# Counting ranks partly on ScalarE, a more even split of row sums, and group matrices six steps ahead in a four-layer graph kernel

## Chip, cores and metric

One Trainium2 chip, one of its cores. The metric is the device time of one execution in microseconds, given as the median of several runs. Float32 inputs and output; TensorE's fp32 matmuls run as two passes in the profile ("x2" for one matmul of the source).

## The reference

Four graph layers over one adjacency matrix `adj` (2708 x 2708, sparse, non-negative) and 2708 nodes with 128 features. Each layer ends in `x = layernorm(x + layer(x))`. Layer 0 is a normalised graph convolution, layer 2 a hyperbolic one, layer 3 sums neighbours over the signs of `adj`. What the change touches is layer 1:

```python
XW = x @ W
s_col, s_row = XW @ a[0, :f], XW @ a[0, f:]
den = exp(leaky_relu(s_row[:, None] + s_col[None, :], 0.01))
num = A @ den
att = where(num != 0, den / num, 0)
H = A @ (att @ XW)
```

`den` depends on two numbers per node only, and `leaky_relu` on the sign of their sum. So once the nodes are sorted by these numbers, a row of `num` differs from its neighbour by few nodes, and a dense product can be replaced by work on groups of sorted nodes.

## The kernel before

Nodes lie in 22 tiles of 128 (`NT`), columns in six blocks (`NB`) of 512, the last one 148 wide. The kernel first reads `adjT` in blocks and does layer 0 (L866), keeping the lower part of the blocks in SBUF (`kept`). Then, block by block, it normalises (`norm_roots`, `normed`), multiplies by the weights (`projected`: TensorE at L1001, ScalarE's copies at L1010 and L1011) and clamps the two numbers per node (`clamped`).

Layer 1 needs the ranks of the nodes. Column tiles 1 to 3 serve as 384 samples (`samples`, first two of them replaced by sentinels). `count` (L1051) compares the samples with one value per partition, on VectorE: for each of 22 node tiles and each of the two numbers `i` one instruction of 128 x 384 adds the comparison's result to `counts[:, i, :]`, and writes the number of hits per node, running, to `counted`. `below_s` is the sum of `counts` over the partitions, as a row and as three columns, by TensorE (L1190 to L1195). From it VectorE finds for every sample how far back a group may reach (`lim`, `prev`, L1209), and in a serial search of 26 steps (L1239) the limits `v` of 26 groups (`GM`). From `v` and the counts per node (`upto`) come one-hot matrices `oh`, TensorE's prefix sums `low` (L1288, L1298), a slot per node (`slot`), and two lists of nodes by group: for each node tile VectorE makes a 128 x 128 one-hot `ohs` (L1326) and TensorE multiplies it into `list` (L1328), first for `i` = 0 (it gives `row_i`, the rows of `adjT` to gather), then for `i` = 1.

Beside that runs the whole sum: `whole_sum` (L803) adds `exp` of one number times every row of `adj`. One row tile is nine narrow matmuls (M = 1) into four column groups of two PSUM banks: blocks 0 to 3 in the first bank, block 4 in four pieces of `q4` = 160 columns (the last 32) and block 5 with 148 in the second. `sum_rows(n)` places `n` of the 22 row tiles between other work on TensorE. Order of the row tiles: those of block 0, of blocks 4 and 5, then 1, 2, 3. The upper blocks were overwritten, so the blocks of rows 0 to 3 are fetched again (`fetch_next`, DMA at L824 on SP's queue) into places that come free when a block of rows has been summed; `x_d` (L1515) and `xw_d` (L1012) are written by the same queue.

`queued(...)` makes the instructions of an engine keep the order in which they are written; elsewhere a scheduler orders them.

Then follows `grouped_attention`: 52 steps `q` (26 groups for each half of the nodes). A step gathers 128 rows (`gather`, GpSimd's indirect DMA, L1415, three steps ahead), multiplies them by a group matrix into `num` (L1464), takes `ln` and `exp` on ScalarE, and adds `xw_g` times `att` into `uacc` two steps later (L1491). The first two partitions carry a running sum from step to step (L1467; the first from `carry0`, L1446). A group matrix is a transpose on TensorE (L707) into one of two PSUM buffers `ps`, which ScalarE empties with a Relu (L708). The same two buffers hold two of every five tiles of `num`. The first three matrices lie in `samples` (`w_first`, `FIRST` = 3), the others in `w_all`, made three steps ahead.

A flag (`good`, `added_up`, `checked`) selects at the end a general path if the data do not fit the assumptions of the fast one.

Of the kernel before, what the change touches and what calls it, by code (L numbers as in the profile page):

```python
# [29 lines left out]
NS = len(SAMPLES) * P  # L30
CAP = 126
FIRST = NS // P
GM = 26
SENTINEL = 1.0e29
EMPTY = -1.0e5
# [17 lines left out]
def tiles(b):  # L53
    return range(b * (BW // P), min(NT, (b + 1) * (BW // P)))
# [3 lines left out]
def kernel(  # L58
# [51 lines left out]
    def iota(name, n, base, step, channel, dt=F32):  # L110
        nc.gpsimd.iota(iota_i[:, :n], pattern=[[step, n]], base=base, channel_multiplier=channel)
        t = const.tile([P, n], dt, tag=name, name=name)
        nc.gpsimd.tensor_copy(t, iota_i[:, :n])
        return t

    iota_b = iota("iota_b", P, 0, 1, 0, BF16)
    part_f = iota("part_f", 1, 0, 1, 1)
    node_z = iota("node_z", NT, -N, P, 1)
# [599 lines left out]
    nc.gpsimd.memset(counts, 0.0)  # L718
    counted = col.tile([P, 2, NT + 1], F32, tag="counted", name="counted")
    nc.gpsimd.memset(counted[:, :, 0:1], 0.0)  # L720

# [60 lines left out]

    e1 = c_tile("e1")
    e2 = c_tile("e2")
    q4 = 160
    order = [0, NB - 2, NB - 1, *range(1, NB - 2)]
    steps = iter([(d, i) for d in order for i in range(len(tiles(d)))])

# [1 line left out]
    sums_of += [(4, i * q4, min(BW, (i + 1) * q4), 32 * i, 1, 0) for i in range(4)]  # L792
    sums_of += [(5, 0, width(5), 96, 1, BW - 3 * q4)]
    tot = []

    def whole_sum(n):
        if not tot:
# [43 lines left out]
    with tc.tile_pool(name="tri", bufs=1) as tp:  # L841
# [174 lines left out]
        def clamped(c):  # L1016
            span = node_span(c)
            with queued(DVE):
                nc.vector.tensor_scalar(
                    rcl[:, :, span].rearrange("p i t -> p t i"),  # L1020
                    rc[:, span, ::-1],
                    RC_MAX,
                    -RC_MAX,
                    op0=ALU.min,
                    op1=ALU.max,
                )
                nc.vector.tensor_copy(cmp_v[:, 0, span], rcl[:, 0, span])
                nc.vector.tensor_scalar(cmp_v[:, 1, span], rcl[:, 1, span], -1.0, None, op0=ALU.mult)
                if c == NB - 1:
                    for i in range(2):  # L1030
                        nc.vector.tensor_add(cmp_v[:, i, span], cmp_v[:, i, span], pad_big[:, span])
            with queued(ACT):
                nc.scalar.activation(e1[:, span], rcl[:, 0, span], AF.Exp)
            if c == 0:
                ps = ps_tile("samples_ps")
                with queued(PE):
                    for q, t in enumerate(SAMPLES):
                        nc.tensor.transpose(
                            ps[:, q * P : (q + 1) * P], rcl[:, 0, t : t + 1].to_broadcast([P, P]), ident
                        )  # L1040
                with queued(DVE):
                    nc.vector.tensor_copy(samples, ps[:, :NS])
                    nc.vector.memset(samples[:, 0:1], -SENTINEL)
                    nc.vector.memset(samples[:, 1:2], SENTINEL)

        def count(c, a=0, b=8):


            with queued(DVE):
                for t, i in itertools.islice(itertools.product(tiles(c), range(2)), a, b):  # L1050
                    nc.vector.scalar_tensor_tensor(  # L1051
                        counts[:, i, :],
                        samples,
                        cmp_v[:, i, t : t + 1],
                        counts[:, i, :],
                        op0=ALU.is_gt,
                        op1=ALU.add,
                        accum_out=counted[:, i, t + 1 : t + 2],
                    )

        def sum_rows(n):
            with queued(PE):
                return whole_sum(n)
# [80 lines left out]
                count(c - 1, 0, 4 if c < NB - 2 else 1)  # L1144
        last_products(NB - 1, 0)
        summed_up(NB - 1)
        count(NB - 3, 1, 3)
        norm_roots(NB - 2)
        norm_roots(NB - 1)
        sum_rows(1)  # L1150
        count(NB - 3, 3, 6)
        normed(NB - 2)
        sum_rows(1)
        normed(NB - 1)
        count(NB - 3, 6)
# [12 lines left out]
    with ctx_keep:  # L1168
# [11 lines left out]
        with tc.tile_pool(name="sort", bufs=1) as st_p:  # L1180
# [4 lines left out]

            lim = srt([P, 2, len(SAMPLES)], "lim")
            prev = srt([P, 2, len(SAMPLES)], "prev")
            below_s = [acc_tile(4 + i, f"below{i}") for i in range(2)]
            with queued(PE):
                nc.tensor.matmul(below_s[0][:, :NS], lhsT=ones_b, rhs=counts[:, 0, :], start=True, stop=True)  # L1190
            for i in range(2):
                if i:
                    nc.tensor.matmul(below_s[i][:, :NS], lhsT=ones_b, rhs=counts[:, i, :], start=True, stop=True)
                for q in range(len(SAMPLES)):
                    nc.tensor.matmul(  # L1195
                        below_s[i][:, NS + q : NS + q + 1],
                        lhsT=counts[:, i, q * P : (q + 1) * P],
                        rhs=ones_b[:, 0:1],
                        start=True,
                        stop=True,  # L1200
                    )

            for i in range(2):
                nc.vector.tensor_scalar(
# [51 lines left out]


            upto = srt([P, 2, NT], "upto")
            nc.vector.tensor_sub(upto, counted[:, :, :NT], counted[:, :, 1:])
# [48 lines left out]
            for i in range(2):  # L1308
# [8 lines left out]
                    )  # L1317
                nc.vector.tensor_reduce(slot[:, i, :], pos[i], AX.X, ALU.add)
                nc.vector.tensor_scalar(slot[:, i, :], slot[:, i, :], 2.0, None, op0=ALU.add)
                ps = ps_tile(f"list{i}")  # L1320
                sum_rows(2)
                for t in range(NT):
                    if i == 0 and t in (8, 16):
                        sum_rows(1)
                    ohs = srt([P, P], f"ohs{i}_{t}", BF16, 10, "ohs")
                    nc.vector.tensor_scalar(ohs, iota_b, slot[:, i, t : t + 1], None, op0=ALU.is_equal)  # L1326
                    with queued(PE):
                        nc.tensor.matmul(  # L1328
                            ps[:, : 6 * GM],
                            lhsT=ohs,  # L1330
                            rhs=val[i][:, t, :, :].rearrange("p n g -> p (n g)"),
                            start=(t == 0),
                            stop=(t == NT - 1),
                        )
# [51 lines left out]
    gs = c_tile("gs", 1)  # L1386

    def added_up():
        below0, okb = (c_tile(n, 1) for n in ("below0", "okb"))
# [12 lines left out]
    def grouped_attention(u_sb, rows_g):  # L1402
        adj_h = adjT.rearrange("k (h w) -> (k h) w", h=2)
        chunks = [(0, BW), (BW, 2 * BW), (2 * BW, HALF)]
        with tc.tile_pool(name="main", bufs=1) as mp:
# [79 lines left out]
            def aggregate(q):  # L1485
# [12 lines left out]
                if g == GM - 1:  # L1498
                    for c, (ca, cb) in enumerate(chunks):
# [474 lines left out]
```

## Time and profile before

| | |
|---|---|
| runs, us | 899.6, 901.1, 905.04; median 901.1 |
| profiled execution, us | 904.86, of which the span 903.1 |
| PE / DVE / ACT / POOL busy | 94% / 61% / 43% / 23% |
| mean granted TensorE clock | 0.973 |
| whole sum, ranks, search and lists | from about 164 to 226 us |
| grouped attention, first to last matmul | from 226.57 to 474 us |
| layers 2 and 3 | from 474 us to the end |

PE is TensorE, DVE VectorE, ACT ScalarE, POOL GpSimd, SP the sync engine whose queue issues most transfers; PEld is TensorE's weight load, which overlaps PE. PEclk is the share of full TensorE clock that was granted, and DMA share the mean busy share of the 16 DMA engines (it can pass 1 where packets overlap). The chain of waits is followed back from the last instruction, each step to what released it; a line of it gives start, duration, engine, tile and source line. "[1.70 <-DMA B]" behind an instruction in a timeline means that the engine was idle for 1.70 us before it and was released by that transfer.

### The profile page before, as it was taken

The numbers are of one execution on the slowest core, as the hardware profiler recorded it, in microseconds if no ns is written. First come the engines' busy times: TensorE is split into PE (matmuls) and PEld (weight loads), VectorE is DVE, ScalarE is ACT, GpSimd is POOL, SyncE is SP. The second block draws the span as 40 slices with busy tenths as digits, with TensorE's granted clock in tenths as the row PEclk, the third lists the DMA queues.
The fourth block names the chain that finished last, engine by engine and source line by source line (L and its number), as shares of the span: only waits on it lengthen the run. The fifth ranks groups of instructions, "written<-read, shape, count | busy, mean of one in ns | idle before, by whom it ended". The sixth has DMA issues, their size and how long they took to land.

```text
span 903.1 us, 9464 instructions
## 1 busy us (share of the span) xinstructions
PE 846.5 (94%) x3268; PEld 430.0 (48%) x3268; DVE 555.2 (61%) x1189; ACT 388.6 (43%) x681; POOL 206.1 (23%) x176
## 2 busy tenths in 40 slices
PE   3699999698899999999999999989999899999996
PEld 3254454335344445444454444534444555555555
DVE  4777548988788888889971226375644564233313
ACT  3776433215787777777761115273332221000000
POOL 5221000101888885776500000000000000000000
PEclk9799999889899999999999999999999999999997
DMA  9995684596596555445534776496764565463410
GB/s 341 366 356 209 120 248 141 180 383 217 185 380 202 161 150 160 141 154 154 154 121 167 267 269 229 133 336 239 264 224 131 208 215 198 144 253 142 162 39 19
DMA packets 95979, 184.30 MB, mean 204 GB/s; under 512 B 6446, under 2 KB 23551, under 8 KB 95668
## 3 DMA queue, kind: packets, MB, share of 16 engines
q1 hardware_dynamic: 85700, 143.82, 46.2%
q0 software_dynamic: 8352, 37.76, 13.0%
q10 hardware_dynamic: 1872, 2.04, 0.7%
q8 instruction: 28, 0.46, 0.2%
q14 instruction: 27, 0.22, 0.1%
HBM read 179.33 MB, written 4.28 MB: 203 GB/s over the span
## 4 chain that ended last, share of the span: by engine, by line
PE 84%; DMA 9%; DVE 4%; ACT 2%; issue 0%; SPq 0%; DVEq 0%; ACTq 0%
PE a L1584 22%; PE num L1464 13%; PE uacc L1491 13%; PE a L1863 12%; PE a L866 9%; PE a L1872 6%; DMA A<-in_adjT_dram 4%; DMA B<-in_adjT_dram 3%; PE t L803 1%; DMA cb<-in_adjT_dram 1%; PE pp L1821 1%; DVE counts L1051 1%; PE mx L1691 1%; DMA rows_g<-in_adjT_dram,row_i 1%; PE su L251 0%
## 5 line engine op out<-in xcount | busy, mean ns | idle before, releaser
L1415 POOL DMA_INDIRECT rows_g<-in_adjT_dram,row_i x52 | 130.8, 2515 | 90.2 <-PE num L1464 41.2
L1469 ACT ACTIVATE ln<-num,inval,occ_l 128x512 f32<-128x512 f32 x156 | 107.4, 724 | 53.4 <-DVE rows_g L1467 49.4
L1863 PE MATMUL a<-cb,ut 128*128 128x512 f32 (+2 forms) x264 | 125.8, 559 | 1.1 <-DMA cb<-in_adjT_dram 1.1
L1491 PE MATMUL uacc<-att,xw_g 128*128 128x512 f32 (+1 forms) x312 | 126.3, 542 | 0.0
L1872 PE MATMUL a<-mask,node 128*128 128x512 f32 (+2 forms) x264 | 120.3, 537 | 0.7 <-DVE mask L1851 0.7
L1464 PE MATMUL num<-rows_g,w_all 128*128 128x512 f32 (+1 forms) x276 | 113.8, 545 | 0.8 <-ACT ln L1469 0.8
L1584 PE MATMUL a<-cb,q_b 128*128 128x512 f32 (+2 forms) x264 | 111.6, 561 | 1.8 <-DMA cb<-in_adjT_dram 1.8
L866 PE MATMUL a<-A,q_b 128*128 128x512 f32 (+2 forms) x264 | 105.9, 549 | 1.6 <-DMA A<-in_adjT_dram 1.6
L1584 PE MATMUL a<-cb,xw 128*128 128x512 f32 (+2 forms) x264 | 107.3, 550 | 0.0
L1467 DVE COPY rows_g<-num 2x512 f32<-2x512 f32 x150 | 88.0, 612 | 15.4 <-PE num L1464 14.1
L1491 PEld LDWEIGHTS uacc<-att,xw_g 128*128 128x128 f32 x312 | 59.1, 190 | 59.0 <-issue 50.0
L1483 DVE TENSOR_TENSOR att<-att,ln 128x1354 f32<-128x1354 f32 x52 | 80.5, 1548 | 2.0 <-ACT ln L1479 2.0
L1464 PEld LDWEIGHTS num<-rows_g,w_all 128*128 128x128 f32 x276 | 49.5, 190 | 54.0 <-issue 38.9
L1872 PEld LDWEIGHTS a<-mask,node 128*128 128x128 f32 (+1 forms) x264 | 48.5, 193 | 49.4 <-issue 47.6
L230 ACT ACTIVATE sq_l<-s 128x512 f32<-128x512 f32 (+1 forms) x11 | 6.6, 604 | 148.2 <-DVE s L1881 116.7
L1479 ACT ACTIVATE ln<-ln 128x1354 f32<-128x1354 f32 x52 | 69.3, 1333 | 1.7
L1851 DVE TENSOR_SCALAR mask<-cb 128x3072 fp32r<-128x3072 f32 (+5 forms) x24 | 33.5, 1395 | 59.1 <-PE a L1872 58.6
L866 PEld LDWEIGHTS a<-A,q_b 128*128 128x128 f32 (+1 forms) x264 | 45.8, 190 | 49.8 <-issue 46.4
L1584 PEld LDWEIGHTS a<-cb,q_b 128*128 128x128 f32 (+1 forms) x264 | 45.1, 192 | 46.9 <-issue 42.8
L1584 PEld LDWEIGHTS a<-cb,xw 128*128 128x128 f32 (+1 forms) x264 | 45.1, 190 | 46.5 <-issue 46.5
L1074 ACT ACTIVATE xw<-A 128x2048 f32<-128x2048 f32 (+3 forms) x36 | 57.0, 1582 | 7.9 <-DMA b_s<-in_b_dram 4.3
L1456 DVE TENSOR_SCALAR att<-q_b,gj_l 128x1354 f32<-128x1354 f32 x52 | 48.2, 927 | 12.7 <-PE uacc L1491 12.6
(445 smaller groups left out, 900.6 us busy)
## 6 DMA issues: line engine op xcount, KB each, us to landing
cb<-in_adjT_dram SPq DMA_DIRECT2D x15, 2816.0 KB
cb<-in_adjT_dram SPq DMA_DIRECT2D x15, 2560.0 KB
A<-in_adjT_dram SPq DMA_DIRECT2D x25, 1024.0 KB
B<-in_adjT_dram SPq DMA_DIRECT2D x18, 1024.0 KB
cb<-in_adjT_dram SPq DMA_DIRECT2D x3, 814.0 KB
cb<-in_adjT_dram SPq DMA_DIRECT2D x3, 740.0 KB
ut<-in_adjT_dram SPq DMA_DIRECT2D x2, 1024.0 KB
A<-in_adjT_dram SPq DMA_DIRECT2D x5, 296.0 KB
```

Source lines behind the costliest of these rows:

```text
L866: nc.tensor.matmul(acc[c][:, :w], lhsT=z[:kw, k, :], rhs=t[:kw, i, :w], start=c not in begun, stop=(d == NB - 1 and k == NT - 1), skip_gro ...
L1074: checks[d, c] = nc.scalar.activation(below[:, :nt, :w], t[:, :nt, :w], AF.Relu, scale=-1.0, accum_out=neg_sum[:, NB * c + d : NB * c + d ...
L1415: got = nc.gpsimd.indirect_dma_start(out=gat[q], out_offset=None, in_=adj_h, in_offset=bass.IndirectOffsetOnAxis(ap=row_i[:, h, g : g + 1] ...
L1464: nc.tensor.matmul(num[:, : cb - ca], lhsT=w, rhs=gat[q][:, ca:cb], start=True, stop=True)
L1467: nc.vector.tensor_copy(gat[q + 1][0:2, ca:cb], num[0:2, : cb - ca])
L1469: nc.scalar.activation(ln_n[q][:, ca:cb], num[:, : cb - ca], AF.Ln, scale=occ_l[:, g : g + 1], bias=inval[:, g : g + 1],)
L1479: nc.scalar.activation(ln_n[q], ln_n[q], AF.Exp, scale=-1.0)
L1483: nc.vector.tensor_mul(att[q], att[q], ln_n[q])
L1491: nc.tensor.matmul(uacc[h][c][:, : cb - ca], lhsT=xw_g[:, g, :], rhs=att[q][:, ca:cb], start=(g == 0), stop=(g == GM - 1),)
L1584: nc.tensor.matmul(acc[:, :w], lhsT=weights[:kw, k, :], rhs=pc[:kw, t, :w], start=(k == 0), stop=(k == NT - 1),)
L1863: nc.tensor.matmul(acc[:, :w], lhsT=edge[:ke, k, :], rhs=pc[:ke, t, :w], start=(k == 0), stop=False, skip_group_check=True,)
L1872: nc.tensor.matmul(acc[:, :w], lhsT=node[:kw, k, j, :], rhs=mask[:kw, t - ma, :w], start=False, stop=(k == NT - 1 and j == 1), skip_group_ ...
```

## The change

Four things, in one diff:

- For node tiles 12 to 21 (blocks from `SIGNS` = 3 on) the counts of the second number (`i` = 1), ten in all, are made by ScalarE: `Sign(samples - v)` into a bf16 tile `sg` (three buffers), with the sum per node in `signed`. TensorE adds each `sg`, times one half, to `below_s[1]` as a row and three columns; the constant by which signs and counts differ falls out of the comparison with `lim`, and is put back in `upto`. The calls of `count`, `sum_rows` and the new `signs` and `signs_summed` are interleaved anew.
- `q4` is 165: the second bank's four column groups get 165 columns each (block 5: 17 + 148).
- The one-hot tiles `ohs` have four buffers instead of ten, and the flag also asks for the largest slot.
- Group matrices: three more before the loop, then six steps ahead instead of three, behind `group_xw` in the text.

```diff
+SIGNS = 3
+    half_b = const.tile([P, 1], BF16, tag="half_b", name="half_b")
+    nc.gpsimd.memset(half_b, 0.5)
...
-    q4 = 160
+    q4 = (N - 4 * BW) // 4
...
+    def below_sum(i, src, w):
+        parts = [(slice(0, NS), w, src)]
+        parts += [(slice(NS + q, NS + q + 1), src[:, q * P : (q + 1) * P], w[:, 0:1]) for q in range(len(SAMPLES))]
+        for at, lhsT, rhs in parts:
+            nc.tensor.matmul(below_s[i][:, at], lhsT=lhsT, rhs=rhs, start=i not in begun_s, stop=True,
+                             skip_group_check=True)
+            begun_s.add(i)
...
+                if c >= SIGNS:
+                    nc.vector.tensor_scalar(neg_v[:, span], cmp_v[:, 1, span], -1.0, None, op0=ALU.mult)
...
-                for t, i in itertools.islice(itertools.product(tiles(c), range(2)), a, b):
+                for t, i in itertools.islice(itertools.product(tiles(c), range(2 - (c >= SIGNS))), a, b):
...
+        def signs(c, a=0, b=4):
+            for t in tiles(c)[a:b]:
+                sg = col.tile([P, NS], BF16, tag="sg", name=f"sg_{t}", bufs=3)
+                with queued(ACT):
+                    nc.scalar.activation(
+                        sg, samples, AF.Sign, bias=neg_v[:, t : t + 1], accum_out=signed[:, t : t + 1]
+                    )
+                sides.append(sg)
+        def signs_summed(n):
+            if not below_s:
+                below_s.extend((acc_tile(4, "below0"), acc_tile(3, "below1")))
+            for _ in range(n):
+                sg = sides.pop(0)
+                with queued(PE):
+                    below_sum(1, sg, half_b.to_broadcast([P, P]))
...
-        count(NB - 3, 1, 3)
+        count(NB - 3, 1, 2)
         norm_roots(NB - 2)
         norm_roots(NB - 1)
         sum_rows(1)
-        count(NB - 3, 3, 6)
+        signs(NB - 3, 0, 2)
+        count(NB - 3, 2)
         normed(NB - 2)
         sum_rows(1)
         normed(NB - 1)
-        count(NB - 3, 6)
         projected(NB - 2)
         projected(NB - 1)
-        sum_rows(2)
+        signs(NB - 3, 2)
+        sum_rows(1)
+        signs_summed(2)
         clamped(NB - 2)
+        signs(NB - 2)
         count(NB - 2)
         clamped(NB - 1)
+        signs(NB - 1)
         count(NB - 1)
+        signs_summed(2)
+        sum_rows(1)
+        with queued(PE):
+            below_sum(1, counts[:, 1, :], ones_b)
+        signs_summed(6)
...
+            nc.vector.tensor_scalar(upto[:, 1, ns:], signed[:, ns:], -0.5, -0.5 * NS, op0=ALU.mult, op1=ALU.add)
...
+                if i:
+                    nc.vector.tensor_reduce(most, slot.rearrange("p i t -> p (i t)"), AX.X, ALU.max)
...
-                    ohs = srt([P, P], f"ohs{i}_{t}", BF16, 10, "ohs")
+                    ohs = srt([P, P], f"ohs{i}_{t}", BF16, 4, "ohs")
...
+        nc.vector.tensor_scalar(fit, most, float(P - 1), None, op0=ALU.is_le)
+        nc.vector.tensor_mul(good, good, fit.to_broadcast([P, NT]))
...
+            with queued(PE, ACT):
+                for g in range(FIRST, FIRST + 3):
+                    group_matrix(w_all, g)
...
                     if q + 3 < GM:
+                        group_xw(q + 3, behind)
+                    if q + FIRST + 3 < GM:
                         with queued(PE, ACT):
-                            group_matrix(w_all, q + 3)
-                        group_xw(q + 3, behind)
+                            group_matrix(w_all, q + FIRST + 3)
```

More of the change, by code (lines that the diff above doesn't have):

```diff
@@ L720 @@
     nc.gpsimd.memset(counted[:, :, 0:1], 0.0)
+    neg_v = col.tile([P, NT], F32, tag="neg_v", name="neg_v")
+    signed = col.tile([P, NT], F32, tag="signed", name="signed")
+    most = col.tile([P, 1], F32, tag="most", name="most")
     xw = const.tile([P, NT, F], F32, tag="xw", name="xw")
@@ L794 @@
     tot = []
+    sides, below_s, begun_s = [], [], set()
+    def below_sum(i, src, w):
+        parts = [(slice(0, NS), w, src)]
+        parts += [(slice(NS + q, NS + q + 1), src[:, q * P : (q + 1) * P], w[:, 0:1]) for q in range(len(SAMPLES))]
+        for at, lhsT, rhs in parts:
+            nc.tensor.matmul(
+                below_s[i][:, at],
+                lhsT=lhsT,
+                rhs=rhs,
+                start=i not in begun_s,
+                stop=True,
+                skip_group_check=True,
+            )
+            begun_s.add(i)
     def whole_sum(n):
@@ L1059, in count @@
                     )
+        def signs(c, a=0, b=4):
[4 more added lines that the diff above has]
+                        sg, samples, AF.Sign, bias=neg_v[:, t : t + 1], accum_out=signed[:, t : t + 1]
+                    )
+                sides.append(sg)
[6 more added lines that the diff above has]
+                    below_sum(1, sg, half_b.to_broadcast([P, P]))
         def sum_rows(n):
@@ L1187 @@
             prev = srt([P, 2, len(SAMPLES)], "prev")
-            below_s = [acc_tile(4 + i, f"below{i}") for i in range(2)]
             with queued(PE):
[L1190 to L1201, printed above, removed]
+                below_sum(0, counts[:, 0, :], ones_b)
             for i in range(2):
@@ L1258 @@
             upto = srt([P, 2, NT], "upto")
-            nc.vector.tensor_sub(upto, counted[:, :, :NT], counted[:, :, 1:])
+            ns = tiles(SIGNS)[0]
+            nc.vector.tensor_sub(upto[:, 0], counted[:, 0, :NT], counted[:, 0, 1:])
+            nc.vector.tensor_sub(upto[:, 1, :ns], counted[:, 1, :ns], counted[:, 1, 1 : ns + 1])
+            nc.vector.tensor_scalar(upto[:, 1, ns:], signed[:, ns:], -0.5, -0.5 * NS, op0=ALU.mult, op1=ALU.add)
             vs = srt([P, GM + 1], "vs")
@@ L1388, in added_up @@
     def added_up():
-        below0, okb = (c_tile(n, 1) for n in ("below0", "okb"))
+        below0, okb, fit = (c_tile(n, 1) for n in ("below0", "okb", "fit"))
+        nc.vector.tensor_scalar(fit, most, float(P - 1), None, op0=ALU.is_le)
+        nc.vector.tensor_mul(good, good, fit.to_broadcast([P, NT]))
         nc.vector.tensor_reduce(below0, neg_sum, AX.X, ALU.add)
```

## The prediction

> **What bounds the kernel now.** I read the page's shares, then the chain of waits in order of time, then a table of 3 us windows, then the timelines of the engines from 160 to 260 us, where all that the diff touches lies.
>
> ```profile
> PE 846.5 (94%) x3268; PEld 430.0 (48%) x3268; DVE 555.2 (61%) x1189; ACT 388.6 (43%) x681; POOL 206.1 (23%) x176
> PE 84%; DMA 9%; DVE 4%; ACT 2%; issue 0%; SPq 0%; DVEq 0%; ACTq 0%
> ```
> TensorE carries the span. VectorE's 61% is an average and says nothing of the stretch in question. The chain there:
> ```profile
> 170.84 4.37 DVE counts L1051 x16
> 175.81 1.78 DVE counts L1051 x6
> 178.80 4.42 PE t L803 x30
> 187.65 12.43 DMA B<-in_adjT_dram
> ...
> 202.19 12.26 DMA B<-in_adjT_dram
> 214.49 0.41 PE t L803 x2
> 217.35 2.45 PE t L803 x30
> 219.80 0.30 PE list L1328 x3
> 220.10 5.41 DMA rows_g<-in_adjT_dram,row_i
> 226.57 3.79 PE num L1464 x4
> ```
> The counts are on the chain from 170.8 to 177.6, then it goes over to the refetched blocks B of the whole sum, and the first gather leaves at 220.10, when the last whole-sum row is through TensorE (row_i was ready at 218.72). The windows (us, then busy PE, PEld, DVE, ACT, POOL, PEclk, DMA share, GB/s):
> ```profile
> 174.00:177.00 3.00, 0.00 (x0) 0.00 (x0) 2.96 (x16) 0.32 (x2) 1.26 (x4) 0.82 1.09 285
> 180.00:183.00 3.00, 3.00 (x32) 1.17 (x24) 2.18 (x10) 0.00 (x0) 0.00 (x0) 0.54 1.05 392
> 186.00:189.00 3.00, 3.00 (x45) 1.25 (x33) 2.82 (x11) 0.60 (x1) 0.00 (x0) 1.00 1.05 387
> 204.00:207.00 3.00, 3.00 (x44) 2.33 (x43) 3.00 (x6) 2.79 (x19) 0.00 (x0) 1.00 1.06 388
> 213.00:216.00 3.00, 2.81 (x35) 1.11 (x38) 2.34 (x15) 0.00 (x0) 0.00 (x0) 1.00 0.12 33
> ```
> From 174 to 213 us the DMA engines are full at about 388 GB/s: 13 blocks of 1 MB and three thin ones. So two things run side by side: VectorE's counts, ranks and group search, and this transfer stream. TensorE waits for the stream at 199.16 (1.70 us), 200.12 (0.51) and 214.49 (0.19); the last landing ends the stream at 214.44.
>
> **What the Trainium skill says.** "ScalarE: Activation LUTs", What ACT_TABLE_LOAD costs: an ACTIVATE with a pointer bias takes about 280 ns plus 0.833 ns per column, 0.60 us at 384. The trace has 302 ns for L1703 (128 columns, no pointer), started every 0.29 us with its accumulator read; adding 256 columns (0.21) and a pointer (0.09) gives 0.60 as well. The same section puts a table switch at 2.66 us; the built order of the changed kernel holds no further table load among the signs and exponentials, so I price none. "TensorE: Matmul & The Clock Gate", Part 1: an idle array falls to half clock and comes back after sustained work. The trace agrees: idle for 4.67 us before 177.73, then PEclk 0.50 to about 182.7, and the 36 matmuls of two rows take 4.49 us instead of 2.52. "DMA: Bandwidth & Descriptors", Rules for kernel authors: all queues share the same 16 engines, so an earlier issue does not widen a full stream; the windows above show it full.
>
> **The change part by part.**
>
> *Counts.* Eight counts start 0.54 us apart (170.81 to 175.13). Ten go, 5.4 us of VectorE, and three small neg_v operations of about 0.1 come. Before 166.7 one count only lengthens an existing wait for ScalarE's roots, so VectorE reaches x (L992) at 167.74 instead of 168.28: 0.54 earlier. The last count ends at about 174.4 instead of 178.1. Next late are the signs: ScalarE is free from 165.7, takes two signs to 166.9, the projection's copies (L1010, L1011) to 170.45, then eight signs of 0.60 with the three buffers of sg handed back by TensorE: I get the last at about 176.3. TensorE's sums cost 0.27 us each at full clock (below at L1190 and three columns take 0.54 at half clock): 2.7 us, in the former idle. So lim starts at about 177.1 instead of 178.35; with a warm TensorE the two rows ahead of prev_ps no longer hold it, and the search (26 steps of 0.655, L1239) starts about 2.2 us earlier and ends at 199.2 instead of 201.4.
>
> *What that buys.* Nothing, I think. Behind the search come oh and low on TensorE, queued behind rows and rb (203.75) that wait for B landings. The end of the stream counts. It starts with B1_2 behind x_d and two writes of xw_d on SP's queue. These start 0.54 earlier, so their bytes are through at about 174.3 instead of 174.8. But B1_2 may only be issued when row 4 of block 0 is summed, and this row now stands behind four sums, of which the fourth needs a sign that needs the first one's buffer: row start 172.45 instead of 171.8, issue 173.4 instead of 172.72. Somewhat above half a microsecond passes from issue to data (x_d: 169.20, DMA busy from about 169.8). Ends between 0.55 earlier and 0.3 later: I take 0.
>
> *Rows dealt 165 instead of 160 and 180.* A row takes 1.21 us (54 matmuls, 3.62) for 692 columns in its two turns; 15 fewer are 0.026, and six rows lie after the stall at 200: 0.15 us gained.
>
> *ohs, four buffers instead of ten.* VectorE makes one in 0.163 to 0.182 us, TensorE's list takes 0.082 (x8 in 0.66), and VectorE restarts 0.28 after a group's first list matmul (214.83 to 215.11). With eight ready the group costs 0.66; with four ready, 0.28 + 4 x 0.175 + 0.2 = 1.2. The first group of list0 grows inside the wait for the landing at 214.44; the second adds 0.5, the last (six) 0.33. So whole sum and gather end 0.83 later. For list1 TensorE has 22 to take: before, twelve were still to be made when it began (219.73 to the copy at 222.53, 2.80 us), now 18, six more at 0.175: 1.05. If VectorE ran at TensorE's full round trip instead it would be far more (rival 3); below nothing it cannot be, as nothing is left out. The added maximum of slot (about 0.2) lies in VectorE's wait.
>
> *Group matrices.* Ahead of the first numerators stood four (L707, L708), now seven: three pass through two PSUM buffers at ScalarE's pace, 0.40 to 0.45 us each. The fourth is out of TensorE at 226.03, so the seventh at about 227.3, against the start of num at 226.57: 0.75. The gather that covers this (landing 225.51, carry copy to 226.53) moves only by the 0.83, while the matrices move by 0.83 + 1.05; the cover is gone. In the loop three steps (20 to 22) lose their matrix: 0.11 each (246.02 to 246.13), and step 21 its stall of 0.28 (num x6 takes 2.72 at 326.13 instead of 2.44): 0.61 gained. Steps 1, 6, 11 and 16 keep theirs, as one matrix per step still takes a PSUM buffer of num. POOL and SP issue in the same order, so nothing moves past their queues.
>
> Sum: 0 - 0.15 + 0.83 + 1.05 + 0.75 - 0.61 = +1.87 us. Two operations of fit come in step 39 of the loop, in VectorE's idle time; behind the loop no engine's order differs, so the rest should shift whole. The profiled execution took 904.86 (span 903.1); with 1.9 more, 906.8. It lies 3.8 above the median of the runs, 901.1; the forecast for a median is 903.0.
>
> **Rivals.**
> Rival 1, not slower: the stream follows its releases. The chain puts the issue at 187.65 on TensorE's rb, which the earlier search and a warm clock bring about 2.2 us forward. If that moved the landings, the sum is 1.87 - 2.2 = -0.3: 900.8. For it: the chain's own edge. Against: share 1.05 and 387 GB/s on both sides of 187.65. It decides from the point where the share dips before that issue; if the earlier start of x_d also moves the stream by its 0.55, 900.2.
> Rival 2: signs take 0.75 instead of 0.60, or the sums hold block 0's last row for another 1.5 us; the full stream then ends that much later: +3.4, 904.5. For it: the buffer ring ties ScalarE and TensorE together. Against: ScalarE is idle for 4.03 and 4.15 us there.
> Rival 3: four buffers run at the round trip. One turn is about 0.175 + 0.25 + 0.2 = 0.63 us; were it not overlapped, 18 + 6 matrices would lose 24 x 0.45 = 10.8 us: 914. Against: 0.63 over four buffers is 0.157, still below VectorE's own pace.
> That the signs are not on ScalarE is excluded: the built order shows all ten.
>
> **How the numbers follow.** Forecast 0.55 (+0.5 to +3), rival 1 0.25, rival 2 0.15, rival 3 0.05. The predicted time is the forecast's, 903.0. The range leaves out rival 3, reaches down past rival 1 and up past rival 2, and takes in the 0.3% by which runs of one kernel differ (899.6 to 905.04): 898.5 to 907.5. A change of 1%, 9 us, is about what a measurement of this kernel can tell from none. Only rival 3 passes it, 0.05; faster by that much, 0.02, would need more than the whole 5.4 us of counts; within 1%, 0.93.
>
> **What would show it.** Right: counts end near 174.4 and lim starts near 177; last B landing within 0.5 us of 214.4; DMA share above 1 throughout; first gather near 221; list1 taking about 3.9 us; first num near 229; one stall fewer in the loop, then everything about 2 us later. Wrong: a landing 2 us earlier (rival 1) or later (rival 2), list1 above 6 us (rival 3), or a difference that first arises after 480 us.

## The result, and the profile after

The changed kernel's median is 906.12 us over 20 runs (903.0 to 908.13), that of the kernel before over 20 runs beside it 904.64 us (899.6 to 906.99). The ratio, which goes by all runs (the two means lie 2.2 us apart, the two medians 1.5), is 1.0024, 95% interval [1.0011, 1.0037]: 2.2 us slower, between 1.0 and 3.3. The forecast was 1.87 us slower. That the median itself lies 3.1 us above the 903.0 of the forecast comes from its base: the kernel before had shown 901.1 over three runs and has 904.64 over twenty. The profiled execution took 904.98 us (span 903.3, clock 0.978), against 904.86 (903.1, 0.973) before: a single pair of profiles doesn't show the 2.2 us, and below it is shown why.

The page of the changed kernel, busy time of the engines and their shares of the chain:

```profile
PE 846.5 (94%) x3308; PEld 428.6 (47%) x3308; DVE 551.8 (61%) x1177; ACT 394.8 (44%) x701; POOL 208.7 (23%) x177
PE 84%; DVE 6%; DMA 6%; ACT 2%; issue 1%; SPq 0%; DVEq 0%; ACTq 0%
```

TensorE has forty matmuls more and the same busy time; 3.4 us went from VectorE and 6.2 came to ScalarE. The chain of waits from 170 to 231 us (start, duration, engine, tile, line):

```profile
171.10 0.63 DVE counts L1077 x2
...
174.32 1.20 ACT sg L1093 x4
...
175.55 1.09 DVE upto L1305
176.64 0.06 DVE lim L1247 x2
...
185.63 13.22 DMA B<-in_adjT_dram
...
198.90 0.65 PE t L827 x2
...
203.99 2.51 PE low L1344 x18
...
210.16 2.43 PE t L827 x30
...
217.86 0.27 DVE ohs L1374
...
221.22 0.38 DVE ohs L1374 x2
...
229.63 0.47 PE gb L711
230.10 2.94 PE num L1514 x4
```

Three things are new. The last signs (`sg`) stand on it where the last counts stood. The second refetch (before: 202.19, 12.26 us) has gone from it: from 198.90 on TensorE's own work is the later one. And VectorE's `ohs` now stands between the lists, and the seventh group matrix (`gb`), not the gather, in front of the first `num`. The windows (us; busy PE, PEld, DVE, ACT, POOL; PEclk, DMA share, GB/s) of the changed kernel:

```profile
174.00:177.00 3.00, 2.18 (x28) 1.11 (x31) 1.39 (x5) 1.63 (x8) 2.43 (x1) 1.00 0.95 335
180.00:183.00 3.00, 2.71 (x39) 1.28 (x43) 2.22 (x9) 0.00 (x0) 0.00 (x0) 1.00 1.05 386
186.00:189.00 3.00, 3.00 (x48) 1.28 (x40) 2.82 (x11) 0.00 (x0) 0.00 (x0) 1.00 1.03 378
...
201.00:204.00 3.00, 3.00 (x22) 1.07 (x15) 3.00 (x6) 0.61 (x3) 0.00 (x0) 0.50 1.05 385
204.00:207.00 3.00, 3.00 (x37) 2.08 (x36) 1.55 (x3) 3.00 (x24) 0.00 (x0) 0.82 1.05 388
213.00:216.00 3.00, 2.74 (x29) 1.22 (x29) 1.87 (x13) 0.00 (x0) 0.00 (x0) 1.00 0.00 0
```

From 177 us on the stream is as full as before. TensorE is warm (at full clock) at 174 to 183, where it had been idle and at half clock, and cold (at half clock for all or part of the time) at 201 to 207, where it had been at 0.63 (first line below, before) and 1.00:

```profile
201.00:204.00 3.00, 3.00 (x24) 1.08 (x23) 2.90 (x7) 0.60 (x1) 0.00 (x0) 0.63 1.05 388
```

**Marks.** Profiles of one program differ in when this stretch begins: VectorE's last `work<-work,b_s,x` of 128x148, which lies ahead of nearly all that is changed, starts between 160.8 and 164.3 us in all these kernels, at 162.5 to 164.1 in three (b1, b2, b3 below) that are the same up to there. So the table counts from that instruction, and takes the last column from the timed runs. "gj_l" is ScalarE's copy ahead of the first group matrix, "loop end" the end of the last matmul into `uacc`. Layers 2 and 3, which follow and which no edit touches, take 425.5 to 429.7 us in these twelve profiles, so a difference of 1 or 2 us between two whole profiles says little.

| kernel | list0 | first gather | list1 done | gj_l | first num | loop end | ratio to before, 95% |
|---|---|---|---|---|---|---|---|
| before | 49.23 | 56.98 | 59.41 | 60.79 | 63.45 | 310.83 | |
| after | 50.84 | 59.62 | 63.30 | 64.59 | 68.21 | 314.34 | 1.0024 [1.0011, 1.0037] |
| b2_ohs4 | 49.48 | 58.29 | 61.89 | 63.17 | 64.93 | 312.02 | 0.9994 [0.9981, 1.0006] |
| b3_six | 49.35 | 56.93 | 59.36 | 60.74 | 64.20 | 312.21 | 1.0008 [0.9995, 1.0021] |
| e3_no_signs | 49.04 | 57.83 | 61.42 | 62.71 | 66.02 | 312.89 | 1.0043 [1.0028, 1.0058] |
| e6_signs_only | 50.80 | 57.97 | 60.40 | 61.79 | 64.18 | 311.29 | 0.9991 [0.9978, 1.0003] |
| e2_gm3 | 49.59 | 58.38 | 62.13 | 63.41 | 65.33 | 312.36 | 1.0003 [0.9989, 1.0017] |
| e5_ohs10 | 51.50 | 58.67 | 61.10 | 62.49 | 65.80 | 312.67 | 0.9992 [0.9976, 1.0007] |
| w1_warm | 48.00 | 58.22 | 61.90 | 63.19 | 66.65 | 314.66 | 1.0020 [1.0008, 1.0033] |
| w2_warm_signs | 48.96 | 58.15 | 60.58 | 61.97 | 64.02 | 311.42 | 0.9991 [0.9975, 1.0007] |
| b1_skip | 49.23 | 56.75 | 59.18 | 60.57 | 63.35 | 309.10 | 0.9985 [0.9974, 0.9997] |
| e7_skip | 49.49 | 57.22 | 59.64 | 61.03 | 64.01 | 310.48 | 0.9968 [0.9955, 0.9981] |

0.001 of the ratio is 0.9 us, and an interval reaches about 1.2 us to each side.

### The profile page after: what moved, and what is told of

Its sections match the earlier page's. It is cut to its first block, busy times and chain, and to the rows that moved or that the text cites. A ratio compares the mean times of both kernels' runs of the same rounds, so it can differ in the third digit from the quotient of the medians.

```text
span 903.3 us, 9582 instructions
## 1 busy us (share of the span) xinstructions
PE 846.5 (94%) x3308; PEld 428.6 (47%) x3308; DVE 551.8 (61%) x1177; ACT 394.8 (44%) x701; POOL 208.7 (23%) x177
## 4 chain that ended last, share of the span: by engine, by line
PE 84%; DVE 6%; DMA 6%; ACT 2%; issue 1%; SPq 0%; DVEq 0%; ACTq 0%
PE a L1638 22%; PE num L1514 13%; PE uacc L1541 13%; PE a L1917 11%; PE a L890 9%; PE a L1926 6%; DMA A<-in_adjT_dram 4%; PE t L827 2%; DMA B<-in_adjT_dram 1%; PE pp L1875 1%; DVE counts L1077 1%; PE low L1344 1%; PE mx L1745 1%; PE su L255 1%; PE st_l L255 0%
## 5 line engine op out<-in xcount | busy, mean ns | idle before, releaser
L1465 POOL DMA_INDIRECT rows_g<-in_adjT_dram,row_i x52 | 133.4, 2566 | 91.2 <-PE list L1376 44.7
```

The costliest lines, as they stand in the source:

```text
L1465: got = nc.gpsimd.indirect_dma_start(out=gat[q], out_offset=None, in_=adj_h, in_offset=bass.IndirectOffsetOnAxis(ap=row_i[:, h, g : g + 1] ...
```

## Experiments

The texts name their theories by letters and say what each expects; letters are used afresh in each set of runs. A further kernel, e1_ohs10, meant to give the signs room for ten buffers of `ohs`, put `sg` into a tile whose slots were overwritten before they were summed; it ran the general path (4039 us) and says nothing on the question. e5_ohs10 takes its place. Each run has its own runs of the kernel before beside it, and its ratio is to those. Every kernel with signs also has the new split of rows.

**e5_ohs10: the changed kernel with ten buffers of `ohs`.** To make room for them, `sg` moves to another pool. That also changes the order in which the scheduler places `upto` and `lim` on VectorE: the first sweep (L1252) starts 14.78 us after the mark instead of 15.03.

```diff
-                sg = col.tile([P, NS], BF16, tag="sg", name=f"sg_{t}", bufs=3)
+                sg = tp.tile([P, NS], BF16, tag="sg", name=f"sg_{t}", bufs=3)
...
-                    ohs = srt([P, P], f"ohs{i}_{t}", BF16, 4, "ohs")
+                    ohs = srt([P, P], f"ohs{i}_{t}", BF16, 10, "ohs")
```

> The changed kernel with ten ohs buffers; the three sg tiles are taken from a pool that is closed by then, which makes the room. Times from VectorE's last s (before 163.12, changed kernel 161.69). Theory A (pacing costs): groups of list0 0.7, 0.7 and 0.6 us instead of 1.32, 1.32 and 1.00; first gather at 58.2 to 58.6 instead of 59.6; list1 2.8 instead of 4.05; loop end 2.3 to 2.9 earlier than the changed kernel's 314.3; median 2 to 3 us below the changed kernel. Theory B (the pacing hides in waits): under 0.5 us.

Measured: 902.83 us over 14 runs, ratio 0.9992 against 1.0024. Its list groups take 0.72, 0.72 and 0.58 us again, and from the first gather to the end of list1 pass 2.43 us, as before, against 3.68. So the four buffers cost the changed kernel 2.9 us (1.0024 less 0.9992, about ±1.8), as much as all that it lost; theory A stands. In the single profile the loop ends only 1.67 us earlier, less than the 2.3 to 2.9 of theory A, since the lists start 0.66 us later.

**e2_gm3: the changed kernel with group matrices as before.**

```diff
-            with queued(PE, ACT):
-                for g in range(FIRST, FIRST + 3):
-                    group_matrix(w_all, g)
...
-                        group_xw(q + 3, behind)
-                    if q + FIRST + 3 < GM:
                         with queued(PE, ACT):
-                            group_matrix(w_all, q + FIRST + 3)
+                            group_matrix(w_all, q + 3)
+                        group_xw(q + 3, behind)
```

> The changed kernel with the group matrices as before the change (four ahead of the first num, then three steps ahead). Theory A: from gj_l to the first num 2.7 us instead of 3.6, but this num runs colder and takes about 4.5 us instead of 3.7, and the loop from its third step to its end is longer by 0.6 us: the loop's end moves by -0.4 to +0.6 us, the total by nothing that can be measured. Theory B: the matrices ahead are a net loss of 1 us or more, the loop ends 1 us earlier.

Measured: 904.05 us over 14 runs, ratio 1.0003. The matrices six ahead cost about 1.9 us (±1.7) where `ohs` has four buffers, which is theory B. From gj_l to the first `num` pass 1.92 us here and 3.62 in the changed kernel: the three further matrices cost 1.7 us once nothing else is waited for there.

**e6_signs_only: the signs, their sums and the new split of rows, without the other two** (the edits of e5_ohs10 and of e2_gm3 together).

> Signs, sums and columns of 165 only: ten ohs buffers, group matrices as before the change. Theory A (the stream of refetched blocks ends the stage, so VectorE's lead is worth nothing): against the changed kernel the pacing goes (2.6) and the front of the loop (1.7 less 0.6), so the loop ends at 310 to 311 after the mark, as before the change (310.8), and the median lies within 1 us of before. Theory B (the lead does pay: the kernel without signs measured 3.9 above before, the changed one 2.2): gather at 55.4 or earlier (before 57.0), median 1.5 us or more below before.

Measured: 902.81 us over 22 runs, ratio 0.9991 [0.9978, 1.0003]: ten counts fewer on VectorE, with the new split of rows, are worth between 2.0 us gained and 0.3 lost, as theory A had it. With e5_ohs10 (0.9992) it also says that matrices six ahead cost nothing measurable where `ohs` has ten buffers.

**e3_no_signs: the kernel before with the three other parts.**

```diff
-    q4 = 160
+    q4 = (N - 4 * BW) // 4
...
-                    ohs = srt([P, P], f"ohs{i}_{t}", BF16, 10, "ohs")
+                    ohs = srt([P, P], f"ohs{i}_{t}", BF16, 4, "ohs")
...
+            with queued(PE, ACT):
+                for g in range(FIRST, FIRST + 3):
+                    group_matrix(w_all, g)
...
-                    if q + 3 < GM:
+                    if q + FIRST + 3 < GM:
                         with queued(PE, ACT):
-                            group_matrix(w_all, q + 3)
+                            group_matrix(w_all, q + FIRST + 3)
```

> The kernel before with only the other parts of the change: columns dealt 165 each, four ohs buffers, group matrices six ahead; no signs, all 44 counts on VectorE. Theory A: search starts 21.2 us after the mark as before; TensorE reaches the row that waits for the landing near 200 later and idles less, so from that landing to list0 it takes 12.2 us instead of 13.6; gather 1.0 to 1.4 later than before (58.0 to 58.4 after the mark, against 59.6 in the changed kernel); loop end 2 to 2.8 later than before. So the total lies between: 1.5 to 2.5 above before, 0.7 to 1.5 below the changed kernel. Theory B: without signs the loss is gone, loop end within 0.7 of before.

Measured: 907.42 us, ratio 1.0043 [1.0028, 1.0058]: without the signs the loss is not smaller. Both theories missed this median: A had it 1.5 to 2.5 us above before, and it is 3.9 (±1.4); B had no loss. By its marks the first `num` comes 2.57 us later than before, the loop's end 2.06, as A had it; the rest of the 3.9 us does not show in this one profile.

**b2_ohs4 and b3_six: each of the two costs alone, in the kernel before.** The edits are the line of `ohs` and the group matrices of the diff above.

> The kernel before with one edit: four buffers of ohs instead of ten. Theory A (the pacing of list0 and list1 is what the change costs, with or without the signs): ratio 1.002 to 1.003, list0 groups 1.2 to 1.3 us each, list1 about 4.05 us instead of 2.80, the first num 1.5 to 2.5 us later. Theory B (four buffers cost only together with matrices six ahead, as the cover of the gather wait is used by both): ratio 1.000 to 1.001.

> The kernel before with one edit: the group matrices as the change has them (three more ahead of the loop, then six steps ahead). No signs, ten buffers of ohs, old split of rows. Theory M (costs add: front +0.75 to 1.1 us in gj_l to the first num, three matrices and one stall fewer in the loop -0.61): ratio 1.000 to 1.001; the 1.0043 of the run with four buffers and matrices six ahead would then need its further 3 us from the two together or from the tail. Theory N (six ahead costs 3 us or more by itself, somewhere behind the first num): ratio 1.003 to 1.005, with the loss between the first num and the loop's end or in layers 2 and 3.

TensorE's timeline in b2_ohs4, lists and first matrices:

```profile
212.90 1.32 PE L1328 MATMUL list<-val,ohs 128*128 128x156 bf16 x8
...
221.34 0.45 PE L1328 MATMUL list<-val,ohs 128*128 128x156 bf16 x4
221.99 3.27 PE L1328 MATMUL list<-val,ohs 128*128 128x156 bf16 x18 [0.21 <-DVE ohs L1326]
...
227.74 0.82 PE L707 MATMUL gb<-ident,gj_l 128*128 128x128 f32 x2 [0.44 <-ACT samples L708]
228.35 4.03 PE L1464 MATMUL num<-rows_g,samples 128*128 128x512 f32 x6
```

Measured: b2_ohs4 904.2 us over 14 runs, ratio 0.9994; b3_six 903.95 over 14, ratio 1.0008. The pacing, TensorE's wait for one-hots that VectorE makes one by one, is there in full (groups 1.32 instead of 0.72, list1 done 2.48 us later), yet the first `num` is only 1.48 later: `num` follows the fourth matrix at once, where it had stood idle for 0.54 us waiting for the gather. In b3_six the lists are as before and the three matrices add 0.80 between gj_l and `num` (3.46 against 2.66), as theory M had it. Theory A of b2_ohs4 falls on the clock and theory B stands; its profile alone (loop end 1.19 later) would have left it open.

Alone, then, neither costs what can be measured (-0.5 and +0.7 us, each ±1.2); together, with the new split of rows, they cost 3.9 (e3_no_signs). The split was not run alone. In the traces it changes a row by 0.01 us (54 matmuls, three rows: 3.69 us before, 3.66 after), so the 3.9 us are not there.

The marks give one reason: ahead of the first `num` there was a cover of 0.74 us (2.66 before, less the 1.92 that four matrices take with no gather to wait for). Each edit alone uses it, the two together can use it once. By the medians the pair costs 3.7 us (±2.1) more than its parts here, and 1.8 (±2.5) more with the signs (2.2 for the changed kernel, with 0.3, -0.7 and -0.8 for e2, e5 and e6). The cover's 0.74 us fits the second figure and is too small for the first. What the rest of that is stays open, and so does why the clock shows nothing of b2_ohs4, whose profile has the first `num` 1.48 and the loop's end 1.19 us later.

**w1_warm and w2_warm_signs: TensorE kept busy in front of the landing near 199 us**, in the changed kernel and in e6_signs_only.

```diff
+                if b == 4:
+                    warm = acc_tile(5, "warm")
+                    with queued(PE):
+                        for _ in range(22):
+                            nc.tensor.matmul(warm, lhsT=ones_b,
+                                             rhs=counts.rearrange("p i n -> p (i n)")[:, :BW],
+                                             start=True, stop=True)
```

> The changed kernel with 22 idle bf16 matmuls of 512 columns (4.7 us at full clock) ahead of the whole-sum row that waits longest for refetched blocks (block b = 4 of that loop); their result is not used. Theory A: PEclk stays 1 from 198 to 207 instead of 0.5; from the landing near 199 to list0 12.2 us or less instead of 13.6, so gather and loop end come 0.9 to 1.4 us earlier (less 0.3 if the last block's landing then holds the next row); total about 1 us lower. Theory B (the stream of blocks alone sets this stage): the gather does not move.

> The kernel with signs only plus the 22 idle matmuls ahead of the waiting row. Theory A: PEclk 1.00 from 198 to 207, list0 starts 48 to 49 after the mark, and then the last landing (about 51.5) holds the row behind the first group, so of the clock's 1.4 us some 0.5 to 0.9 remains: gather 55.5 to 56.5, loop end 309.5 to 310.3, median 0.5 to 1.5 below before. Theory B (the landing alone sets it): gather as in the kernel with signs only.

A window of w1_warm, to hold against the 0.50 of the same stretch above:

```profile
201.00:204.00 3.00, 3.00 (x32) 1.62 (x25) 3.00 (x6) 1.96 (x10) 0.00 (x0) 1.00 1.05 385
```

In its profile the lists start 2.84 us earlier than in the changed kernel and the gather leaves 1.40 earlier, as theory A had it. The median, which it put 1 us lower, doesn't follow: 906.44, ratio 1.0020 against 1.0024. Its profiled execution loses the lead again where the loop starts (step 0's `num` takes 4.50 us instead of 3.69, the end of step 1's 3.10 instead of 1.68, and the loop's end is at 314.66, as in the changed kernel). So the cold clock is shown in the profile, and that it costs the median anything is not. w2_warm_signs (0.9991, as e6_signs_only) shows what stands next when the lists are neither paced nor cold; its chain:

```profile
201.22 12.27 DMA B<-in_adjT_dram
...
213.54 0.41 PE t L827 x2
213.95 0.65 PE list L1387 x8
...
218.83 0.31 PE list L1387 x3
219.13 4.94 DMA rows_g<-in_adjT_dram,row_i
```

The last landing holds the row, the row the list, the list the gather. TensorE got to the lists 1.84 us earlier than in e6_signs_only and the gather left at 58.15 against 57.97: no gain (theory B). In e6_signs_only itself the chain runs through TensorE's own work from the landing near 198 us to the lists, and not through the last landing: there a cold TensorE comes to the same place as late. In these two profiles one or the other holds the gather near 58, and that is why the signs, which end the search earlier, buy next to nothing.

**e7_skip and b1_skip: three matrices more ahead of the loop, none at steps 0 to 2, then three ahead as before**, in e5_ohs10 and in the kernel before.

```diff
-                    if q + FIRST + 3 < GM:
+                    if q > 2 and q + 3 < GM:
                         with queued(PE, ACT):
-                            group_matrix(w_all, q + FIRST + 3)
+                            group_matrix(w_all, q + 3)
```

> Signs, ten ohs buffers, and six group matrices before the loop but none in steps 0 to 2, from step 3 on three steps ahead. If the stall of 2.1 to 2.3 us before the second chunk of step 1 comes from the matrix that shares the two PSUM buffers with num, it goes, and the loop's first two steps are 1 to 2 us shorter; the front costs 0.8 (six matrices instead of four): loop end 0.3 to 1.2 before that of the kernel with signs only. If the stall has another cause (ln and exp of step 0 on ScalarE), the loop ends 0.8 later than that kernel's.

> The kernel before with one edit: three more group matrices ahead of the loop, none at steps 0 to 2, and from step 3 on one per step, three ahead as before. No signs, ten buffers of ohs. Theory S (the best version so far gains from this edit alone: no matrix takes a PSUM buffer of num at step 1, where the stall is 2.1 to 2.3 us, and three more matrices lie mostly in the wait for the first gather): ratio to before about 0.998, 1.5 to 2 us faster; in the trace no stall between num of steps 0 and 2, gj_l to the first num about 3.0 us against 2.66. Theory T (the signs must lead, or the edit shows nothing): ratio 1.000, within 0.5 us of before.

TensorE's timeline of e7_skip at the loop's start:

```profile
225.88 0.87 PE L711 MATMUL gb<-ident,gj_l 128*128 128x128 f32 x2 [0.20 <-ACT samples L712]
226.54 8.88 PE L1514 MATMUL num<-rows_g,samples 128*128 128x512 f32 x18
235.40 2.51 PE L1541 MATMUL uacc<-att,xw_g 128*128 128x512 f32 x6
```

The same stretch of the changed kernel:

```profile
229.90 3.69 PE L1514 MATMUL num<-rows_g,samples 128*128 128x512 f32 x6
233.42 0.27 PE L711 MATMUL gb<-ident,gj_l 128*128 128x128 f32 x1
233.53 1.02 PE L1514 MATMUL num<-rows_g,samples 128*128 128x512 f32 x2
236.84 1.68 PE L1514 MATMUL num<-rows_g,samples 128*128 128x512 f32 x4 [2.28 <-ACT w_all L712]
```

Three steps of `num` go through without a stop; with a matrix (`gb`) in step 0 TensorE stands still for 2.28 us in step 1, since `num` waits for the PSUM buffer until ScalarE has emptied the matrix, behind two `ln` and the `exp` of step 0. e7_skip takes 901.39 us over 22 runs, ratio 0.9968 [0.9955, 0.9981]: 2.9 us faster than before, and the best of all; its loop ends 0.81 us ahead of that of e6_signs_only, as expected. b1_skip, the same edit alone, takes 902.19 over 22, ratio 0.9985 [0.9974, 0.9997]: 1.4 us faster, near the 1.5 to 2 of theory S. It is the first use of the change's own idea that pays: matrices early, but not one in each of the first steps. What e7_skip has beyond b1_skip, 1.5 us ±1.6, would be the signs and the split, and no run settles it.

Not all that the early matrices win is kept. In b1_skip `num` of step 3 starts 3.15 us earlier than before, counted from the mark (75.10 against 78.25), but the loop ends only 1.73 earlier. At step 8 TensorE stands still for 0.99 us, where it had no stall before (in e7_skip 1.29), and the chain leads to that step's gather:

```profile
249.73 10.05 DMA rows_g<-in_adjT_dram,row_i
...
260.58 1.97 ACT ln L1469 x3
...
262.60 2.54 PE num L1464 x6
```

## Why the prediction was right, and where it was not

The sum was right, +1.87 against +2.2 [1.0, 3.3], and its mechanism is borne out: the signs buy next to nothing (e6_signs_only), four buffers of `ohs` and matrices six ahead cost (e5_ohs10, e2_gm3), and in the trace the cover ahead of the first `num` is gone, as it said. The sizes of several terms were off in the profile, some up and some down, so that the sum came out nearer than its terms is in part luck.

*Counts: right that they buy nothing, but 2.2 us of lead were 1.4.* The signs are on ScalarE as priced: 0.60 us each, two waits for a buffer, the last starting at 174.83, which on the clock of before (1.43 later at the mark) is 176.26 against 176.3 forecast. ScalarE's timeline:

```profile
170.46 0.62 ACT L1093 ACTIVATE sg<-samples,neg_v 128x384 bf16<-128x384 f32 x1 [0.61 <-PE below L810]
...
173.52 0.61 ACT L1093 ACTIVATE sg<-samples,neg_v 128x384 bf16<-128x384 f32 x1 [0.46 <-PE below L810]
...
174.83 0.60 ACT L1093 ACTIVATE sg<-samples,neg_v 128x384 bf16<-128x384 f32 x1
```

What fell short is the lead at `lim`. The first sweep behind it (L1252) starts 15.03 us after the mark, before 15.42: 0.39 earlier, where 1.25 was forecast (178.35 less 177.1). The counts left on VectorE do not hold it, although they start 0.65 to 0.67 us apart, not the 0.54 of before (five such steps, 0.6 us). VectorE's timeline after:

```profile
169.77 0.62 DVE L1077 SCALAR_TENSOR_TENSOR counts<-samples,cmp_v,counts 128x384 bf16<-128x384 f32 x1
...
170.44 0.62 DVE L1077 SCALAR_TENSOR_TENSOR counts<-samples,cmp_v,counts 128x384 bf16<-128x384 f32 x1
...
175.55 1.09 DVE L1305 TENSOR_SCALAR upto<-signed 128x10 f32<-128x10 f32 x1 [1.53 <-ACT sg L1093]
```

The last count ends at 173.8 (175.2 on the clock of before; forecast 174.4), and VectorE then stands idle until the last sign. Two things come after that. TensorE's last sums end 1.35 us after the last sign starts, where the forecast left 0.8. And `upto`, 128 x 10, takes 1.09 us: it ends 0.04 us behind a MEMSET on GpSimd that began at 174.17 and took 2.43. Where `upto` stands behind `lim` (e5, e6, e7 and w2) the sweep starts at 14.78 or 14.79, 0.25 earlier.

Most of the lead comes from the other half of the step, TensorE no longer cold ahead of `prev_ps` (VectorE's wait for it is 0.64 us instead of 1.48), and the search starts 1.43 us earlier, not 2.2. The first refetch is issued 10.88 us after the mark, before 9.60: 1.28 later, where 0.7 was forecast. The landing near 199 us moved by only 0.21 (37.21 after the mark, before 37.00), and the stream's end did not move, as forecast: no engine waits for a transfer between 213 and 216 us, and its share falls about 50 us behind the mark in both.

*A term that was missing: the lead lets TensorE cool.* What was earlier by 1.4 us met the same landing, so TensorE was idle longer ahead of it (1.08 us busy of the 3 at 195 to 198, before 2.46). In this profile it then did the work from that landing to the first list in 13.63 us (198.90 to 212.53) instead of 12.23 (200.12 to 212.35). The prediction had cited the idle array's half clock for the stretch at 177 us and did not ask where the lead would leave it idle next. It differs from one execution to the next. Programs that are the same up to the lists took for this stretch 13.63 us (the changed kernel) and 12.34 (e2_gm3), and 13.18, 13.62 and 12.27 (e5, e6 and e7); the five without signs all took 12.2 to 12.4. That agrees with the Trainium skill, "TensorE: Matmul & The Clock Gate", Part 1, where the window that sets the clock runs freely and the number of cold matmuls varies from run to run. As w1_warm showed, the median doesn't need this term.

*Four buffers: right in kind, too small by a third in the profile.* TensorE's timeline before:

```profile
212.35 0.72 PE L1328 MATMUL list<-val,ohs 128*128 128x156 bf16 x8
...
216.77 0.58 PE L1328 MATMUL list<-val,ohs 128*128 128x156 bf16 x6
...
219.73 2.76 PE L1328 MATMUL list<-val,ohs 128*128 128x156 bf16 x22
```

And after:

```profile
212.53 1.32 PE L1376 MATMUL list<-val,ohs 128*128 128x156 bf16 x8
...
215.05 1.32 PE L1376 MATMUL list<-val,ohs 128*128 128x156 bf16 x8
...
217.58 1.00 PE L1376 MATMUL list<-val,ohs 128*128 128x156 bf16 x6
...
220.94 0.45 PE L1376 MATMUL list<-val,ohs 128*128 128x156 bf16 x4
221.60 3.35 PE L1376 MATMUL list<-val,ohs 128*128 128x156 bf16 x18 [0.21 <-DVE ohs L1374]
...
229.63 0.47 PE L711 MATMUL gb<-ident,gj_l 128*128 128x128 f32 x1 [0.20 <-ACT w_all L712]
```

Groups of eight grew by 0.60 us (forecast 0.54, from 0.66 to 1.2), the six by 0.42 (0.33), list1 to 4.05 from 2.80, 1.25 (1.05). That the first group would vanish in the wait for the landing held only in part: 0.19 us of idle time was all the wait that the timeline of before showed there, and from this group to the next passed 0.54 us more than from that to the third (212.35 to 214.83, and to 216.77). b2_ohs4, without signs or cold clock, has the gather 1.31 us later where 0.83 was written, and list1 done 2.48 later where the two terms make 1.88. The clock's 2.9 ±1.8 (e5_ohs10) does not tell these two apart.

*Group matrices: 0.75 forecast, 0.96 found* from gj_l to the first `num` (3.62 less 2.66), 0.80 in b3_six. *The loop: -0.61 forecast and found.* From `num` of step 3 to the loop's end pass 232.58 us before (241.37 to 473.95) and 231.97 after (244.06 to 476.03). The other profiles agree: 232.58 to 232.68 in the four others with matrices three ahead all along, 231.97 or 231.98 in the four others with six. The stalls of the early steps stayed.

*The split of rows: 0.15 forecast, about 0.06 found*, as a row became 0.01 us shorter and not 0.026.

*The rivals.* Rival 1 fell: the release that it named came 0.59 us earlier (185.63 and 187.65, each from its mark), the landings did not follow, and the share stayed at 1.03 to 1.08 from 177 us to shortly before the stream's end. Rival 2 fell: signs 0.60, sums 0.24 us apart, and the 1.28 us by which block 0's last row held the first refetch did not reach the stream's end. Rival 3 fell: 18 `list` matmuls behind VectorE took 3.35 us, 0.19 each, VectorE's own pace and not the round trip.

*What one profile shows.* Without the signs (e3_no_signs) the first `num` is 2.57 us later, and the forecast's three terms ahead of it sum to 2.63: 0.83, 1.05 and 0.75. With the loop's -0.61 they make 2.0, which is near the 2.2 us of the changed kernel; but the medians of e3_no_signs itself say 3.9 ±1.4, so that the clock follows the terms one by one is not shown. The changed kernel's own profile shows another path to its end: first `num` 4.76 later on the mark's clock, the loop's end 3.51 later, but the mark itself 1.43 earlier and layers 2 and 3 shorter by about 1.9. Those layers hold nothing that was changed. In one place there TensorE is idle for 2.2 to 2.3 us near 596 us in both, and ran the four matmuls behind it at half clock before (3.20 us) and at full clock after (1.88).

## What to carry to other kernels

A gap ahead of the bounding engine can be spent once: two edits that are each free beside it are to be priced together (here the gap explains a part of what they cost), in the state in which the other one has used it up. When a stretch is brought forward to meet a transfer that doesn't move, ask what the engine does in the new gap, and give room in SBUF taken by one part of a change (here 2.25 KB of `sg`) the price of the buffers that it displaces. Work moved earlier in a loop pays when it leaves the steps that are short of a shared PSUM buffer, not when each step still holds one of it.

## What the runs showed of the hardware

- VectorE's counts of 128x384 started 0.54 us apart while they went to two targets in turn, and 0.65 to 0.67 apart when each added to the target of the one before it: fewer instructions, each later by 0.12 us.
- ScalarE ran `Sign` between its exponentials and logarithms with no further table load in the trace (32 loads of 1.28 us before and after): 0.60 us for 128x384 with a bias per partition, as often as every 0.60 us with the read of its accumulator.
- With idle times of 2.2 to 2.3 us at the same place, TensorE came back at full clock in one profile and at half clock in another. Stretches of the same program between a landing and the lists differed by 1.3 us, so differences of that size were read from medians.
- VectorE's `upto` (TENSOR_SCALAR of 128x10, SBUF to SBUF) took 0.19 to 1.11 us in the seven kernels with signs named in the table, and in each it ended 0.03 or 0.04 us behind GpSimd's MEMSET, however far ahead of that end it had started. `lim` (TENSOR_SCALAR from PSUM) and the TENSOR_TENSOR parts of `upto` took 0.15 to 0.17 us during that MEMSET (e5, e6, e7, w2). Why the one waits and the others don't no run shows.
